# A selective scan's units doubled to half an image: in place in SBUF, its running product in four PSUM banks, the products for y gathered once a step

## The chip, the cores and the metric

The kernel runs on one NeuronCore of a Trainium2 chip. A core has a matrix engine (PE, with its weight loads shown as PEld), a vector engine (DVE), a scalar engine (ACT), a general engine (POOL) and SP, which here only issues DMA transfers. Each engine works through its own instructions in order and waits at semaphores for the others. SBUF holds the working tiles, PSUM (eight banks of 2 KB for each partition) takes what PE writes. The metric is the device time of one execution in microseconds, the median over runs. The kernel before takes 4079.44 us (three runs, 4076.0 to 4084.84).

## The reference

The input is x of shape 32 x 96 x 56 x 56, float32. Layer 0 is a ConvNeXt block (7x7 depthwise convolution, normalisation, MLP, residual). Layer 1 is a selective scan; it is the part that the change touches:

```python
x = conv_general_dilated(x, conv_w, ..., feature_group_count=C) + conv_b   # 5x5 depthwise
xs = silu(x).reshape(B, C, L)                     # L = 56*56 = 3136 tokens an image
x_dbl = einsum('kd,bdl->bkl', x_proj_w, xs)
dts, Bs, Cs = x_dbl[:, :R], x_dbl[:, R:R+N], x_dbl[:, R+N:]       # R = 6, N = 4
delta = softplus(einsum('dr,brl->bdl', dt_w, dts) + dt_b[None, :, None])
log_dA = maximum(delta[:, :, None, :] * A[None, :, :, None], LOG_EPS)      # A = -exp(A_logs)
P = exp(cumsum(log_dA, axis=-1))
dB_u = delta[:, :, None, :] * Bs[:, None, :, :] * xs[:, :, None, :]
hs = P * cumsum(dB_u / maximum(P, EPS), axis=-1)
y = einsum('bdnl,bnl->bdl', hs, Cs) + xs * Ds[None, :, None]
```

All 96 channels times 4 states are scanned along the 3136 tokens of each of 32 images.

## The kernel before

The kernel has four parts, one after the other: the first convolution, the MLP, the second convolution, and the scan, each with its own pools of tiles. The second convolution leaves silu's result in DRAM as `conv2_d`, laid out channel, image row, then all images' columns. The scan reads it from there.

In the scan, a **step** `k` is a chunk of tokens of one image and a **unit** `i` is a third of a step: 32 channels times 4 states fill the 128 partitions, so a step has NG = 3 units. A chunk is CH = 784 tokens, a quarter of an image, and NI = 4 images go side by side: steps 0 to 3 are the first quarters of images 0 to 3, steps 4 to 7 their second quarters. That makes 128 steps and 384 units. A group of NI steps shares one load of xs.

What is done for a step and its units, by function:

- `load` (L477, SP): xs for the next group, 96 partitions; each piece in DRAM is one image row of NI images, 4 x 56 floats, 896 bytes.
- `delta_in` (L495, PE) and `delta` (L506, ACT): the product of xs with a 96 x 96 matrix into PSUM, then softplus into the first half of tile `du`. Softplus needs another table in ACT than the exponential.
- `delta_x` (L523, POOL; L524, SP): delta times xs into the second half of `du`, and `du` stored to DRAM (`du_d`).
- `rows_bc` (L513, PE; L518, ACT), `spread_bc_in` (L532, PE), `spread_bc` (L542 and L543, ACT): the rows of B and C, and then B and C spread over all partitions as tiles `bt` and `ct`.
- `spread_du` (L552, SP): a unit's delta and delta*x are read back from `du_d`, each channel's row onto four partitions, as tile `rep` (two halves, four buffers).
- `decay` and `clamp` (L559, L565, L566, ACT): exp(delta*A) and two instructions that keep it above 1e-9, from `rep` into tile `da`.
- `drive` (L570, POOL): delta*x*B from `rep` into tile `u`.
- `scan` (L578, L582, L583, L587, DVE): the running product of `da` (a scan over the tokens) into PSUM tile `pv`, its last column kept in `carry_p` for the image's next chunk, the smaller of it and 1 times `u`, and the second scan into tile `hs`.
- `weigh` (L597, L599, POOL): `hs` times C into tile `hc`, and the last column of `hs` kept in `carry_h`.
- `gather` (L495 and L609, PE): D*x and the sums over the states, two matrix products a unit, into PSUM tile `py`; `store` (L618, ACT; L619, SP): `py` copied to SBUF and stored as y.

PSUM is divided into two banks for `pv`, two pairs of banks that `pz`, `pn` and `pk` take in turn (tag `bc`), and one pair for `py`.

The order on every engine is written out by hand: the loop at L631 to L667 records all instructions, and `pin` keeps them in that order on their engine. In the pass for unit `i`, `rep` is asked for unit `i + 6`, the decay and drive are done for unit `i + 3`, the scan for `i`, weigh and gather for `i - 1`. `load` stands at place 9 of a group's 12 passes, two groups ahead; softplus for a whole group stands at place 1, `delta_x` at places 1 to 4.

Of the kernel before, what the change touches and what calls it, by code (L numbers as in the profile page):

```python
# [21 lines left out]
N, R = 4, 6  # L22
# [5 lines left out]
CH = 784  # L28
NI = 4
NCH = L // CH  # L30
BK = CH // 2
# [9 lines left out]
def convnext_then_scan_kernel(  # L41
# [31 lines left out]
    du_d = dram.tile([B * NCH, C, 2 * CH], F32, name="du_d")  # L73
# [367 lines left out]
    with tc.tile_pool(name="sc", bufs=2) as pool, tc.tile_pool(  # L441
        name="sc_k", bufs=1, space=PSUM
    ) as ps_k, tc.tile_pool(name="sc_ps", bufs=2, space=PSUM) as ps_bc, tc.tile_pool(
        name="sc_y", bufs=1, space=PSUM
    ) as ps_y:
        pin = tc.keep_in_program_order

        pv = ps_k.tile([128, 1024], F32, name="pv")
        nc.vector.memset(pv, 0.0)
        zero = pv[:, 1023:1024].to_broadcast([128, CH])  # L450
# [9 lines left out]
        ready: dict = {}  # L460
        done: dict = {}
        pys: dict = {}
        pzs: dict = {}
        pks: dict = {}
        carry_p = pool.tile([128, NI * NG], F32, name="carry_p", bufs=1)
        carry_h = pool.tile([128, NI * NG], F32, name="carry_h", bufs=1)

# [4 lines left out]

        def load(p):
            b, q = place(p * NI)
            hq = H // NCH
            xt = pool.tile([C, hq, NI * W], F32, name=f"xs_{p}", tag="xs", bufs=3)
            pin(nc.sync.dma_start(  # L477
                xt,
                conv2_d[:, q * hq : (q + 1) * hq, b * W : (b + NI) * W],
            ))  # L480
            xts[p] = xt

        def tokens(k, s):

            p, i = divmod(k, NI)
            hh = H // NCH // 2
            rows = slice(s * hh, (s + 1) * hh) if s is not None else slice(None)
            return xts[p][:, rows, i * W : (i + 1) * W]
# [4 lines left out]
        def product(ps, wt, k, start=True, stop=True):  # L493
            for s in range(2):
                pin(nc.tensor.matmul(  # L495
                    half(ps, s), lhsT=wt, rhs=tokens(k, s), start=start, stop=stop
                ))

        def delta_in(k):
            pzs[k] = ps_bc.tile([128, 2, 512], F32, name=f"pz_{k}", tag="bc")  # L500
            product(pzs[k][:C], wd_t, k)

        def delta(k):
            du = pool.tile([C, 2, CH], F32, name=f"du_{k}", tag="du", bufs=5)
            o, z = two(du[:, 0, :]), pzs.pop(k)[:C, :, :BK]
            pin(nc.scalar.activation(o, z, AF.Softplus, bias=dtb_t, scale=1.0))  # L506
            dus[k] = du

        def rows_bc(k):

            pn = ps_bc.tile([128, 2, 512], F32, name=f"pn_{k}", tag="bc")
            for i in range(4):
                pin(nc.tensor.matmul(  # L513
                    half(pn[32 * i : 32 * i + 32], 0), lhsT=bcw_t, rhs=tokens(k, i % 2),
                    start=True, stop=True, tile_position=(0, 32 * i),
                ))
            bn = pool.tile([128, BK], F32, name=f"bn_{k}", tag="bn", bufs=5)
            pin(nc.scalar.copy(bn, pn[:, 0, :BK]))  # L518
            bns[k] = bn

        def delta_x(k):
            d, u = (dus[k][:, i, :].rearrange("p (h w) -> p h w", w=W) for i in range(2))
            pin(nc.gpsimd.tensor_mul(u, d, tokens(k, None)))  # L523
            pin(nc.sync.dma_start(du_d[k], dus.pop(k).rearrange("p i t -> p (i t)")))  # L524

        def spread_bc_in(k):

            bn = bns.pop(k)
            pk = [ps_bc.tile([128, 2, 512], F32, name=f"pk_{k}_{i}", tag="bc") for i in range(2)]
            for i in range(4):  # L530
                rows = slice(32 * i, 32 * i + 2 * N)
                pin(nc.tensor.matmul(  # L532
                    pk[i // 2][:, i % 2, :BK], lhsT=pick_t[rows], rhs=bn[rows],
                    start=True, stop=True, tile_position=(32 * i, 0),
                ))
            pks[k] = pk

        def spread_bc(k):
            pk = pks.pop(k)
            bt = pool.tile([128, CH], F32, name=f"bt_{k}", tag="bt", bufs=2)  # L540
            ct = pool.tile([128, CH], F32, name=f"ct_{k}", tag="ct", bufs=3)
            pin(nc.scalar.copy(two(bt), pk[0][:, :, :BK]))  # L542
            pin(nc.scalar.copy(two(ct), pk[1][:, :, :BK]))  # L543
            bts[k], cts[k] = bt, ct

        def spread_du(i):
# [3 lines left out]
            du = du_d[k, g * DG : (g + 1) * DG, :]  # L550
            src = bass.AP(du.tensor, du.offset, [du.ap[0], [0, N], *du.ap[1:]])
# [3 lines left out]
        def decay(i):  # L555

            da = pool.tile([128, CH], F32, name=f"da_{i}", tag="da", bufs=5)
            g = i % NG
            pin(nc.scalar.activation(da, reps[i][:, 0, :], AF.Exp, scale=a_t[:, g : g + 1]))  # L559
            ready[i] = da  # L560

        def clamp(i):

            da = ready[i]
            pin(nc.scalar.activation(da, da, AF.Relu, bias=lift_t[:, 0:1], scale=1.0))  # L565
            pin(nc.scalar.activation(da, da, AF.Identity, bias=lift_t[:, 1:2], scale=1.0))  # L566

        def drive(i):
            ut = pool.tile([128, CH], F32, name=f"u_{i}", tag="u", bufs=5)
            pin(nc.gpsimd.tensor_mul(ut, reps.pop(i)[:, 1, :], bts[i // NG]))  # L570
            ready[i] = ready[i], ut

        def scan(i):
            k, g = divmod(i, NG)
            (b, q), col = place(k), k % NI * NG + g
            da, ut = ready.pop(i)
# [9 lines left out]
            ht = pool.tile([128, CH], F32, name=f"hs_{i}", tag="hs", bufs=3)  # L586
# [3 lines left out]
            done[i] = ht  # L590

        def weigh(i):
            k, g = divmod(i, NG)
            q, col = place(k)[1], k % NI * NG + g
            hc = pool.tile([128, CH], F32, name=f"hc_{i}", tag="hc", bufs=3)
            ht = done.pop(i)
            pin(nc.gpsimd.tensor_mul(hc, ht, cts[k]))  # L597
            if q < NCH - 1:
                pin(nc.gpsimd.tensor_copy(carry_h[:, col : col + 1], ht[:, CH - 1 : CH]))  # L599
            done[i] = hc  # L600

        def gather(i):
            k, g = divmod(i, NG)
            if g == 0:
                pys[k] = ps_y.tile([C, 2, 512], F32, name=f"py_{k}", tag="py")
                product(pys[k], dsm_t, k, stop=False)
            hc = done.pop(i)
            for s in range(2):
                pin(nc.tensor.matmul(  # L609
                    pys[k][g * DG : (g + 1) * DG, s, :BK], lhsT=sel_t,  # L610
                    rhs=hc[:, s * BK : (s + 1) * BK], start=False, stop=True,
                    tile_position=(0, g * DG),
                ))

        def store(k):
            b, q = place(k)
            yt = pool.tile([C, CH], F32, name=f"y_{k}", tag="y")
            pin(nc.scalar.copy(two(yt), pys.pop(k)[:, :, :BK]))  # L618
            pin(nc.sync.dma_start(out[b, :, q * CH : (q + 1) * CH], yt))  # L619

        def at_step(i, fn):
            if i % NG == 0 and 0 <= i // NG < steps:
                fn(i // NG)
# [7 lines left out]
        for i in range(-10, units + 3):  # L631

            p, at = divmod(i + 10, PER)
            first = p * NI
            if at == 9 and p + 2 < PC:
                load(p + 2)
            at_unit(i + 6, spread_du)
            if i >= 2:
# [73 lines left out]
```

## Time and profile before

| | us |
|---|---|
| median of three runs | 4079.44 (4076.0 to 4084.84) |
| the profiled execution's own time | 4078.9 |
| its span, first to last instruction | 4077.1 |
| first xs load of the scan / first scan on DVE / end of the last scan | 2069.4 / 2099.3 / 4065.4 |
| DVE, POOL, ACT, PE busy between 2600 and 3000 us | 372, 343, 324, 301 of 400 |

In the page's second part the span is cut into 40 equal slices, each digit the busy share in tenths; the scan is the last 20. PEclk is the clock that PE was granted, in tenths of full speed. A group's line gives the source line, the engine, the operation, what it writes and reads with shapes, how often, then busy microseconds in all and the mean in nanoseconds of one, then the idle time of the engine just before them and what ended most of it. A table by stretches gives the busy time of PE, PEld, DVE, ACT and POOL in each stretch (number of instructions in brackets), then the granted clock from 0 to 1, the DMA engines' mean share and their rate in GB/s. A matrix product in float32 shows as two matmul instructions.

### The profile page before, as it was taken

What the parts mean: (1) busy time and instruction counts of PE and PEld (TensorE: products, weight loads), DVE (VectorE), ACT (ScalarE), POOL (GpSimd) and SP (SyncE); (2) the same over time, 40 slices, a digit from 0 to 9 for tenths busy, and PEclk for the clock granted to TensorE, in tenths of its full rate; (3) what the DMA queues carried; (4) which work ended last, traced back from release to release, by engine and by line L of the source; (5) the groups of instructions that cost most, each with busy time, mean ns of one, the idle gap of its engine ahead of it and who ended that gap; (6) DMA issues with size and microseconds to landing.
All of it is one profiled execution on the core that took longest, in us unless ns stands there. A gap on an engine that the chain in (4) does not pass through costs nothing. (4 is left out here: it accounts for less than half of the span.)

```text
span 4077.1 us, 45318 instructions
## 1 busy us (share of the span) xinstructions
PE 3340.8 (82%) x15370; PEld 1487.1 (36%) x15370; DVE 2415.9 (59%) x2181; ACT 2417.0 (59%) x2773; POOL 1965.1 (48%) x1661
## 2 busy tenths in 40 slices
PE   7999994988989888999967777777777777777775
PEld 5777771333333333666632222222222222222221
DVE  5666652222222211000039999999999999999998
ACT  3555542333333332444468877877878788787885
POOL 2333320000000000111148888888888888888886
PEclk9999996999999999999978787777778877777877
DMA  5555543444444443777777777777777777777763
GB/s 153 168 167 166 166 141 106 139 133 127 138 134 137 133 136 96 205 222 222 222 234 238 241 239 230 241 234 234 238 234 234 237 238 234 238 234 235 238 218 126
DMA packets 290731, 785.88 MB, mean 193 GB/s; under 512 B 54084, under 2 KB 161924, under 8 KB 290500
## 3 DMA queue, kind: packets, MB, share of 16 engines
q1 hardware_dynamic: 247684, 667.21, 53.4%
q0 software_dynamic: 42816, 115.77, 9.0%
q8 instruction: 122, 2.00, 0.2%
q14 instruction: 109, 0.89, 0.1%
HBM read 550.06 MB, written 232.64 MB: 192 GB/s over the span
## 5 line engine op out<-in xcount | busy, mean ns | idle before, releaser
L609 PE MATMUL py<-hc,sel_t 128*32 128x392 f32 x1536 | 736.2, 626 | 333.2 <-POOL hc L597 333.2
L597 POOL TENSOR_TENSOR hc<-hs,ct 128x784 f32<-128x784 f32 x384 | 721.6, 1879 | 294.9 <-DVE hs L587 290.7
L570 POOL TENSOR_TENSOR u<-rep,bt 128x784 f32<-128x784 f32 x384 | 716.5, 1866 | 11.2 <-DMA rep<-du_d 11.1
L356 ACT ACTIVATE g<-ph,b1p_t 128x896 f32<-128x896 f32 x336 | 320.4, 1004 | 632.9 <-PE ph L346 632.9
L269 PE MATMUL ps<-xq,wt 120*112 120x448 f32 x1536 | 581.2, 539 | 13.3 <-POOL xq L264 13.3
L578 DVE TENSOR_TENSOR_SCAN pv<-da,carry_p,pv 128x784 f32<-128x784 f32 x288 | 534.1, 1854 | 30.9 <-DVE hs L587 0.9
L587 DVE TENSOR_TENSOR_SCAN hs<-da,carry_h,pv 128x784 f32<-128x784 f32 x288 | 531.8, 1846 | 31.1 <-DVE pv L583 1.4
L365 PE MATMUL po<-g,w_t 128*32 128x448 f32 x4032 | 454.1, 588 | 98.9 <-DVE o L377 98.9
L386 POOL DMA_DIRECT2D block_d<-o x84 | 57.7, 689 | 952.5 <-DVE o L377 949.0
L269 PEld LDWEIGHTS ps<-xq,wt 120*112 120x112 f32 x1536 | 429.4, 280 | 164.7 <-POOL xq L264 13.5
L609 PEld LDWEIGHTS py<-hc,sel_t 128*32 128x32 f32 x1536 | 165.3, 129 | 862.3 <-POOL hc L597 490.8
L346 PE MATMUL ph<-h,w1r_t 32*128 32x448 f32 x4032 | 434.2, 558 | 45.0 <-DVE h L328 43.7
L416 PE MATMUL ps<-xp,wt 120*128 120x432 f32 (+1 forms) x1152 | 425.2, 533 | 18.2 <-DMA xp<-block_d 18.2
L583 DVE SCALAR_TENSOR_TENSOR pv<-pv,u 128x784 f32<-128x784 f32 x384 | 377.4, 983 | 41.5 <-DVE carry_p L582 0.9
L566 ACT ACTIVATE da<-da,lift_t 128x784 f32<-128x784 f32 x384 | 364.3, 949 | 12.9
L565 ACT ACTIVATE da<-da,lift_t 128x784 f32<-128x784 f32 x384 | 364.0, 948 | 11.8
L559 ACT ACTIVATE da<-rep,a_t 128x784 f32<-128x784 f32 x384 | 363.9, 948 | 4.9 <-DMA rep<-du_d 4.5
L328 DVE TENSOR_TENSOR h<-h,r 128x896 f32<-128x896 f32 x84 | 91.7, 1092 | 441.0 <-DMA h<-conv_d 423.2
L495 PE MATMUL py<-xs,dsm_t 96*96 96x392 f32 x512 | 311.2, 752 | 45.2 <-ACT y L618 44.9
L416 PEld LDWEIGHTS ps<-xp,wt 120*128 120x128 f32 x1152 | 289.7, 252 | 153.8 <-issue 21.8
L428 ACT ACTIVATE st<-ps,c2b_t 56x896 f32<-56x896 f32 x192 | 204.5, 1065 | 214.7 <-issue 210.3
L377 DVE SCALAR_TENSOR_TENSOR o<-po,b2r_t,x 128x448 f32<-128x448 f32 x168 | 112.3, 680 | 355.8 <-PE po L365 339.1
(84 smaller groups left out, 3318.0 us busy)
## 6 DMA issues: line engine op xcount, KB each, us to landing
rep<-du_d SPq DMA_DIRECT2D x384, 784.0 KB
du_d<-du SPq DMA_DIRECT2D x128, 588.0 KB
xt<-in_x_dram SPq DMA_DIRECT2D x192, 196.0 KB
h<-conv_d SPq DMA_DIRECT2D x84, 448.0 KB
x<-in_x_dram SPq DMA_DIRECT2D x336, 112.0 KB
block_d<-o POOLq DMA_DIRECT2D x84, 448.0 KB, 11.7
xp<-block_d SPq DMA_DIRECT2D x192, 196.0 KB
conv_d<-st POOLq DMA_DIRECT2D x96, 392.0 KB, 4.5
```

The lines of the kernel that those rows point to most:

```text
L269: nc.tensor.matmul(ps[:, j, :PQ].rearrange("p (i r) -> p i r", i=BI), lhsT=wv[:KR, t], rhs=xq[:KR, j, :, t : t + W2], start=(t == 0), stop ...
L346: pin(nc.tensor.matmul(phs[i // 2][:, i % 2, :HALF], lhsT=w1r_t[rows, d, f * 128 : (f + 1) * 128], rhs=hts[n, d][rows, s * HALF : (s + 1) ...
L365: pin(nc.tensor.matmul(po[CB * i : CB * i + CB, :HALF], lhsT=w2_t[:, f, CB * d : CB * d + CB], rhs=gts[n, s, f, i // 2][:, i % 2], start=( ...
L416: nc.tensor.matmul(ps[:, j, :PQ].rearrange("p (i r) -> p i r", i=BI)[:, :, lo:hi], lhsT=wv[:KR, t], rhs=xt[:KR, j].rearrange("p (i r) -> p ...
L565: pin(nc.scalar.activation(da, da, AF.Relu, bias=lift_t[:, 0:1], scale=1.0))
L566: pin(nc.scalar.activation(da, da, AF.Identity, bias=lift_t[:, 1:2], scale=1.0))
L570: pin(nc.gpsimd.tensor_mul(ut, reps.pop(i)[:, 1, :], bts[i // NG]))
L578: pin(nc.vector.tensor_tensor_scan(run, da, zero, carry_p[:, col : col + 1] if q else 1.0 / EPS, ALU.mult, ALU.add))
L583: pin(nc.vector.scalar_tensor_tensor(run, in0=run, scalar=1.0, in1=ut, op0=ALU.min, op1=ALU.mult))
L587: pin(nc.vector.tensor_tensor_scan(ht, da, run, carry_h[:, col : col + 1] if q else 0.0, ALU.mult, ALU.add))
L597: pin(nc.gpsimd.tensor_mul(hc, ht, cts[k]))
L609: pin(nc.tensor.matmul(pys[k][g * DG : (g + 1) * DG, s, :BK], lhsT=sel_t, rhs=hc[:, s * BK : (s + 1) * BK], start=False, stop=True, tile_p ...
```

## The change

CH becomes 1568 tokens (half an image) and NI becomes 2. So there are 64 steps and 192 units, groups of two steps and six units, and 32 groups as before.

- The running product `pv` takes four PSUM banks. The other four are two pairs that `pz`, `pn`, `pk` and now also `py` take in turn (`bank_pair`).
- The decay's three instructions write over `rep`'s first half, the drive over its second, weigh over `hs`; tiles `da`, `u` and `hc` go. `hs` has five buffers. `rep` keeps four.
- PE's and ACT's work on a step is split into halves of 784 tokens (HT) for softplus, `delta_x`, the spreads and y. `du` is stored in halves; `du_d` holds delta and delta*x of a step each in one row.
- `gather` no longer runs per unit. When a step's three units are done it makes, for each half, D*x and the six sums of the three units, whose outputs lie in different groups of columns, and stores y.
- The loop's distances change: `rep` is asked for unit `i + 3`, decay for `i + 2`, drive for `i + 1`; `load` is one group ahead at place 3 of 6; all four softplus stand at place 0, `delta_x` at places 0 to 3. Within a pass ACT's order is decay, spreads, rows, softplus, y; POOL's is weigh, drive, `delta_x`.
- A row of xs in DRAM is now 2 x 56 floats, 448 bytes.

```diff
-CH = 784
-NI = 4
+CH = 1568
+NI = 2
...
-        pv = ps_k.tile([128, 1024], F32, name="pv")
+        pv = ps_k.tile([128, 2048], F32, name="pv")
...
+        def bank_pair(name):
+            return psum.tile([128, 2, 512], F32, name=name, tag="bc")
...
+        def delta_x(k, h):
+            du = dus.pop((k, h))
+            d, u = (du[:, i, :].rearrange("p (h w) -> p h w", w=W) for i in range(2))
+            pin(nc.gpsimd.tensor_mul(u, d, tokens(k, h, 2)))
+            pin(nc.sync.dma_start(du_d[k][:, :, h * HT : (h + 1) * HT], du))
...
         def decay(i):
-            da = pool.tile([128, CH], F32, name=f"da_{i}", tag="da", bufs=5)
-            g = i % NG
-            pin(nc.scalar.activation(da, reps[i][:, 0, :], AF.Exp, scale=a_t[:, g : g + 1]))
-            ready[i] = da
+            g, da = i % NG, reps[i][:, 0, :]
+            pin(nc.scalar.activation(da, da, AF.Exp, scale=a_t[:, g : g + 1]))
...
         def drive(i):
-            ut = pool.tile([128, CH], F32, name=f"u_{i}", tag="u", bufs=5)
-            pin(nc.gpsimd.tensor_mul(ut, reps.pop(i)[:, 1, :], bts[i // NG]))
-            ready[i] = ready[i], ut
+            ut = reps[i][:, 1, :]
+            pin(nc.gpsimd.tensor_mul(ut, ut, bts[i // NG]))
...
-            ht = pool.tile([128, CH], F32, name=f"hs_{i}", tag="hs", bufs=3)
+            ht = pool.tile([128, CH], F32, name=f"hs_{i}", tag="hs", bufs=5)
...
+        def gather(k, h):
+            py = bank_pair(f"py_{k}_{h}")
+            for s in range(2):
+                pin(nc.tensor.matmul(
+                    half(py[:C], s), lhsT=dsm_t, rhs=tokens(k, 2 * h + s, 4),
+                    start=True, stop=False,
+                ))
+            for s in range(2):
+                cols = slice((2 * h + s) * BK, (2 * h + s + 1) * BK)
+                for g in range(NG):
+                    pin(nc.tensor.matmul(
+                        py[g * DG : (g + 1) * DG, s, :BK], lhsT=sel_t,
+                        rhs=hss[k * NG + g][:, cols], start=False, stop=True,
+                        tile_position=(0, g * DG),
+                    ))
...
+            pin(nc.scalar.copy(two(yt), py[:C, :, :BK]))
+            pin(nc.sync.dma_start(out[b, :, q * CH + h * HT : q * CH + (h + 1) * HT], yt))
...
+        for i in range(-12, units + 2):
+            p, at = divmod(i + 8, PER)
+            g = i % NG
+            if at == 3 and p + 1 < PC:
+                load(p + 1)
+            at_unit(i + 3, spread_du)
+            at_unit(i - 1, weigh)
+            at_unit(i + 2, decay)
+            at_unit(i + 1, drive)
+            if g == 1 and 0 <= (i + 2) // NG < steps:
+                for h in range(2):
+                    spread((i + 2) // NG, 0, h)
+            if g == 2 and 0 <= (i + 1) // NG < steps:
+                for h in range(2):
+                    spread((i + 1) // NG, 1, h)
+            if g == 2 and 0 <= (i + 4) // NG < steps:
+                rows_bc((i + 4) // NG)
+            if 0 <= p < PC and at == 0:
+                for j, h in halves:
+                    delta_in(p * NI + j, h)
+                    delta(p * NI + j, h)
+            if 0 <= p < PC and at < 4:
+                j, h = halves[at]
+                delta_x(p * NI + j, h)
+            at_unit(i, scan)
+            if g == 0 and 0 <= i // NG - 1 < steps:
+                for h in range(2):
+                    gather(i // NG - 1, h)
```

Lines of the changed kernel that the prediction speaks of: L476 loads xs, L501 is softplus, L507 delta*x, L521 the copy of the rows, L545 the read of `rep`, L551 the exponential, L564, L569 and L573 the scan's long instructions, L605 the store of y.

## The prediction

> **What bounds the kernel now.** I read the page first (busy tenths by slice), then a table by stretches of the scan stage, then the groups of instructions, then the timeline of one stretch, and last a few short stretches for the DMA rate and the clock. The change touches only the scan stage, which begins at 2069.4 us with the first load of xs and lasts to the end.
>
> ```profile
> DVE  5666652222222211000039999999999999999998
> ACT  3555542333333332444468877877878788787885
> POOL 2333320000000000111148888888888888888886
> PEclk9999996999999999999978787777778877777877
> ...
> 2600.00:3000.00 400.00, 301.20 (x962) 93.90 (x961) 372.31 (x301) 324.19 (x382) 343.30 (x250) 0.78 0.75 235
> ```
>
> From slice 21 on DVE is at 9 in every full slice. The table row (busy of PE, PEld, DVE, ACT, POOL, then granted clock, DMA share, GB/s) says 93% DVE, 86% POOL, 81% ACT, 75% PE at a clock of 0.78. The groups tell what the other 7% of DVE are:
>
> ```profile
> L578 DVE TENSOR_TENSOR_SCAN pv<-da,carry_p,pv 128x784 f32<-128x784 f32 x288 | 534.1, 1854 | 30.9 <-DVE hs L587 0.9
> L587 DVE TENSOR_TENSOR_SCAN hs<-da,carry_h,pv 128x784 f32<-128x784 f32 x288 | 531.8, 1846 | 31.1 <-DVE pv L583 1.4
> L583 DVE SCALAR_TENSOR_TENSOR pv<-pv,u 128x784 f32<-128x784 f32 x384 | 377.4, 983 | 41.5 <-DVE carry_p L582 0.9
> L566 ACT ACTIVATE da<-da,lift_t 128x784 f32<-128x784 f32 x384 | 364.3, 949 | 12.9
> L518 ACT COPY bn<-pn 128x392 f32<-128x392 f32 x128 | 58.5, 482 | 61.8 <-PE pn L513 61.8
> L542 ACT COPY bt<-pk 128x784 f32<-128x784 f32 x128 | 102.1, 797 | 44.1 <-PE pk L532 44.1
> ```
>
> DVE's idle time is 0.1 us between its own instructions; apart from one first wait of 33 us on ACT, no other engine holds it. First scan at 2099.30, last scan ends at 4065.45: 1966 us for 384 units, 5.12 each, 61.4 for twelve (four images' chunks before, a "round" of six units after). So POOL, ACT and PE may be late by some microseconds and it costs nothing. The question is whether that stays so.
>
> **The change, part by part.** A round after the change is six units: two images, half an image each; there are 32.
>
> *DVE.* A unit has the same four instructions over twice the tokens. If the 157 ns of the 128x1 carry copy (L582) are the fixed part, 784 more tokens cost 1.66 us in a scan and 0.83 in L583: 3.48 + 1.81 + 3.48 + 0.08 (half the units copy a carry) = 8.85, with 0.32 of gaps 9.17. Bounds: all fixed cost kept, 10.24; both fixed parts fully saved as taken. Six make 55.0, so DVE alone would gain 6.4 a round, 206 us.
>
> *POOL.* By its 194 ns copy as the fixed part a product over 1568 tokens costs 3.54 (bound: 3.73). Twelve, four products for u of 1.86, three carries: 50.5 a round, under 55.0.
>
> *ACT.* Copies from PSUM grow from 482 ns at 392 tokens to 797 at 784, so 784 tokens more cost about 0.65. The three decay instructions take 2.82 from start to start now, so 4.78 then (bound, doubled: 5.64). Per round: six decays 28.7, eight bt/ct copies at 0.70 5.6, two bn 1.4, four y 2.8, four softplus 3.3, two table loads at 1.30 2.6: 44.4. By sums DVE stays the bound. But ACT's order is pinned, and each of its waits below is longer than in the kernel before, since what it waits for now stands in a closed circle.
>
> *Wait 1, xs.* After SP has stored y of both halves (L605), it issues xs (L476) and only then the next rep (L545), and the queue works in order. ACT comes to that rep after one decay and two bt copies, 6.2 us after the y copy that released SP. SP's side: 2.3 of latency (the stage's first xs load took 8.04 in the chain of waits, 5.7 of it moving), 0.9 for the store of y in front, then xs, then rep. The rates, from stretches with one kind of transfer each (xs alone, then rep alone):
>
> ```profile
> 2072.00:2077.00 5.00, 0.00 (x0) 0.00 (x0) 0.00 (x0) 0.00 (x0) 0.00 (x0) 0.50 1.13 214
> 2095.00:2101.00 6.00, 0.00 (x0) 0.00 (x0) 1.70 (x1) 4.15 (x5) 3.13 (x2) 0.50 1.02 421
> ```
>
> xs now has rows of 896 bytes and moves at 214 GB/s; rep, rows of 6272, at 421. On 16 engines that is 67 ns and 238 ns a packet, a line of 39 ns + 0.032 ns per byte. xs rows shrink to 448 bytes (NI goes from 4 to 2), 168 per engine: 53 ns each, 8.9 us a load. Bounds: 5.7 if only the bytes count, 11.3 if only the packets count; I take the line, which uses both rows. rep is 1.6 MB, 3.8. Sum 2.3 + 0.9 + 8.9 + 3.8 = 15.9; ACT waits 9.7 (6.5 to 12.1). In the kernel before, rep is asked for six units ahead and ACT's wait on it is 4.9 us in all. Now the rep tile holds da and u in place, is free only after the last scan, and is asked for three units ahead; that lead of 27 us covers a plain rep (6.1) but is of no use while SP stands at the store of y.
>
> [...]
>
> *Wait 2, PE.* All products share two bank pairs, so PE may begin pn only after a ct copy, pz only after a bt copy, and ACT needs the result a copy or a table load later. Their price hangs on the clock:
>
> ```profile
> 3008.40:3017.88 9.48, 9.48 (x20) 2.55 (x20) 8.82 (x8) 6.52 (x8) 6.71 (x6) 0.50 0.49 157
> 3017.88:3024.71 6.83, 2.60 (x8) 0.67 (x8) 6.38 (x6) 3.92 (x5) 5.45 (x6) 1.00 1.10 283
> 3024.71:3031.54 6.83, 6.83 (x17) 1.89 (x16) 6.06 (x5) 5.35 (x7) 4.83 (x3) 0.50 0.79 266
> 3031.54:3045.20 13.66, 10.82 (x43) 3.93 (x41) 12.83 (x9) 13.29 (x15) 11.51 (x7) 1.00 0.57 170
> 3045.20:3052.00 6.80, 5.11 (x13) 2.03 (x14) 6.38 (x5) 5.29 (x8) 6.80 (x5) 0.50 0.95 336
> ```
>
> The clock is 0.50 or 1.00. It rises after a stretch in which PE was busy throughout, here after 9.5 and 6.8 us, and falls after one with 38% or with idle at its end. Matmul instructions follow each other at 0.33 us at full clock (four take 1.5) and 0.65 at half (2.8); with several column groups beside each other 24 took 2.34. After the change a round has some 24.6 us of PE work at full clock (four pz at 1.31, two pn at 1.55, eight pk at 0.68, four of D's products at 1.31, four times six y sums at 1.4, three columns beside each other), 49 at half, in three bursts, each begun after idle time. So I count bursts at 0.50 for their first 8.5 us:
> - bn: pn takes 3.1 + 0.3, ACT arrives after 0.7: 2.7, twice (full clock 1.0).
> - y: from pn's end D's products and the sums twice, 5.4 for the first half at 0.50, 2.7 for the second: 8.3 with 0.2 to the end, ACT there after bn, a decay and y, 6.2: 2.1, twice (0 to 4.9).
> - softplus: four pz of 2.62 behind the bt copy against 0.81 each: 0.9 + 3 x 1.8 = 6.3 (full clock 1.2).
>
> [...] The rows here show 9.5 and 6.8 us of unbroken work before the rise, so I keep the sum at 8.5.
>
> *What is queued behind.* POOL's product for u (L507) stands behind softplus, which stands behind a decay and two bt copies of the same step on ACT; POOL's next weigh, drive and so L569 on DVE stand behind it. With ACT late DVE pays at L569 and at L564.
>
> *Hidden.* SP issues 480 transfers for 672. du is stored as two rows of 3136 bytes, four units ahead. hs has five buffers and comes free with the y products, well before L573 needs it.
>
> *Start and end.* xs of the second round is now issued ahead of the first rep: 3.3 for the slower first load and about 9 for the second, so ACT's first decay moves from 2096 to 2108. The end after the last y copy stays: 4069.8 to 4077.1, 7.3.
>
> *Sum*, along ACT from its first decay: work 32 x 44.4 = 1421; xs 30 x 9.7 = 291 (two loads lie ahead of the steady rounds); bn 64 x 2.7 = 173; y 64 x 2.1 = 134; softplus 31 x 6.3 = 195: 2214. 2108 + 2214 + 7 = 4329, with the 1.8 between span and time (4077.1, 4078.9) 4331. The profiled execution is 0.5 below the median, 4079.44.
>
> **Rivals.**
> - *DVE stays the bound* (faster). It ties with today when ACT's waits are 16.4 a round (61.4, less 18 us of start and end over 32 rounds, less 44.4); I count 25.6. PE at full clock gives 9.7 + 2.0 + 1.2 = 12.9, 1421 + 291 + 64 + 37 = 1813 and so 3930; with xs at 5.7 us DVE's 55.0 decides: 4079 - 206 + 18 = 3891. For it: sums of all engines are below 55. Against: PE's work per round falls to 40% at full clock, and stretches of 38% end at 0.50.
> - *ACT bound, but cheap rows or a mixed clock*: xs at 5.7 takes 96 off, 4235; a clock that is up half the time takes off half of what full clock would (401), 4130.
> - *Half clock throughout and 11.3 a load*: y waits 4.9 (+179), xs +72: 4582. Decays at their bound would add 165 to any of these (5.2 a round).
> - *No change*: only by a balance of these.
>
> **How the numbers follow.** Forecast 4331, chance 0.55 for 4255 to 4430; half clock 0.17; cheap rows or mixed clock 0.18; DVE bound 0.08; within 0.2% (about what a measurement tells from no change, 8 us) 0.02. Slower: 0.55 + 0.17 + 0.18 = 0.90, faster 0.08. The range leaves out the DVE case and the upper half of the half-clock one: 4130 to 4490.
>
> **What would show it.** DVE busy falls to about 80% in the stage, with waits at L569 on POOL and L564 on ACT; POOL waits at L507 for softplus by some 10 us a round; ACT waits at L551 for rep some 9 us a round, at L501 for pz 6, at L521 for pn 3 twice. Granted clock in the stage below 0.78. Wrong would make it: a clock near 1.0, a rep that lands before ACT asks, or decay instructions far from 1.6 us.

## The result, and the profile after

| | before | after |
|---|---|---|
| median | 4082.14 us (4 runs) | 4185.49 us (4184.54 to 4191.64, 4 runs) |
| ratio | | 1.0258, 95% interval 1.0240 to 1.0275 |
| the profiled execution's own time, span | 4078.9, 4077.1 | 4191.64, 4189.8 |
| a round (six of the new units, twelve of the old) | 61.4 us | (4175.1 - 2117.3)/32 = 64.3 us |

The forecast, 4331, had the right sign and the right engine, but its size was wrong: 252 us more than before, where 103 were measured. The measured time lies in the stated range of 4130 to 4490, but below the 4255 to 4430 that stood for the forecast's own sum.

The busy tenths of the 40 slices, of the changed kernel:

```profile
DVE  5666651222222221000068778787787887877878
ACT  3555542333333333444466676766767667667675
POOL 2333320000000000111167878778777787787877
PEclk9999997999999998999966666666666666666666
```

Where DVE stood at 9 throughout, it is now at 7 or 8. The table by stretches, same columns as in the prediction (PE, PEld, DVE, ACT, POOL, clock, DMA share, GB/s):

```profile
2600.00:3000.00 400.00, 237.99 (x870) 77.54 (x866) 326.43 (x131) 275.93 (x232) 306.50 (x118) 0.65 0.69 228
```

No engine is over 82%: this is a kernel that waits. The groups of instructions over the whole kernel, with what ended the idle time before each, say who waits for what:

```profile
L551 ACT ACTIVATE rep<-rep,a_t 128x1568 f32<-128x1568 f32 x192 | 307.7, 1603 | 218.3 <-DMA rep<-du_d 215.5 <-DVE hs L573 2.4
L604 ACT COPY y<-py 96x784 f32<-96x784 f32 x128 | 103.2, 806 | 179.5 <-PE py L597 177.7
L521 ACT COPY bn<-pn 128x784 f32<-128x784 f32 x64 | 52.0, 812 | 142.2 <-PE pn L515 142.2
L501 ACT ACTIVATE du<-pz,dtb_t 96x784 f32<-96x784 f32 x128 | 116.3, 909 | 98.7 <-PE pz L493 97.8 <-issue 0.9
```

ACT pays 215.5 us for `rep`, 177.7 for y's sums, 142.2 for `bn` and 97.8 for Softplus. It is busy 1111 of the 1600 us between 2200 and 3800, 44.7 a round, 1430 in 32. Work and waits (`rep` without the 13.6 ahead of the first decay) make 2049 of the 2074 us from the first decay (2112.4) to the end of the last y copy (4186.4); the rest, 25 us, is what is left between its 1209 instructions, 21 ns for each. So the chain that I had summed is the one that sets the end. DVE's idle time is passed on to it: 293 us at L569 behind POOL, 65 at L564 behind ACT.

One round in the timeline (start, duration, engine, line; in brackets the idle time and what ended it), first the Softplus burst, then the queue of SP around xs:

```profile
3018.40 7.71 PE L493 MATMUL pz<-xs,wd_t 96*96 96x392 f32 x16 [4.54 <-ACT bt L537]
3021.36 0.91 ACT L501 ACTIVATE du<-pz,dtb_t 96x784 f32<-96x784 f32 x1 [1.01 <-PE pz L493]
3022.35 1.84 POOL L507 TENSOR_TENSOR du<-du,xs 96x784 f32<-96x784 f32 x1 [14.30 <-ACT du L501]
...
3031.13 1.80 DVE L569 SCALAR_TENSOR_TENSOR pv<-pv,rep 128x1568 f32<-128x1568 f32 x1 [9.59 <-POOL rep L557]
...
3043.39 3.75 SPq L605 DMA_DIRECT2D out_dram<-y  x2
3045.99 0.81 ACT L604 COPY y<-py 96x784 f32<-96x784 f32 x1 [2.62 <-PE py L597]
...
3047.24 0.38 SPq L476 DMA_DIRECT2D xs<-conv_d  x1
3047.71 3.47 SPq L545 DMA_DIRECT2D rep<-du_d  x1
...
3059.49 1.60 ACT L551 ACTIVATE rep<-rep,a_t 128x1568 f32<-128x1568 f32 x1 [6.52 <-DMA rep<-du_d]
```

The reader is to see two chains. ACT's first Softplus is late, POOL has stood 14.30 us at the product that needs it, and DVE stands 9.59 us for POOL. And SP sends the y store, xs and `rep` in that order: from the end of the y copy (3046.80) to the decay that needs `rep` it takes 12.69 us, 6.52 of them idle on ACT.

### The profile page after: what moved, and what is told of

Same layout as the page of the kernel before. It is cut to its first block, busy times and chain, and to the rows that moved or that the text cites. A ratio compares the mean times of both kernels' runs of the same rounds, so it can differ in the third digit from the quotient of the medians.

```text
span 4189.8 us, 41783 instructions
## 1 busy us (share of the span) xinstructions
PE 3145.8 (75%) x15370; PEld 1451.1 (35%) x15370; DVE 2272.1 (54%) x1413; ACT 2278.5 (54%) x2133; POOL 1867.9 (45%) x1085
## 4 chain that ended last, share of the span: by engine, by line
POOL 18%; issue 17%; DVE 8%; DMA 5%; ACT 2%; PE 1%; POOLq 0%; DVEq 0%; SPq 0%; ACTq 0%
POOL rep L557 9%; POOL hs L584 6%; DMA rep<-du_d 4%; DVE hs L573 3%; POOL du L507 3%; DVE pv L564 3%; DVE pv L569 2%; ACT rep L551 1%; ACT rep L552 1%; ACT ct L537 1%; DMA xs<-conv_d 0%; PE pz L493 0%; PE py L597 0%; PE py L590 0%; POOL carry_h L583 0%
## 5 line engine op out<-in xcount | busy, mean ns | idle before, releaser
L584 POOL TENSOR_TENSOR hs<-hs,ct 128x1568 f32<-128x1568 f32 x192 | 672.7, 3504 | 50.9 <-ACT ct L537 32.6
L557 POOL TENSOR_TENSOR rep<-rep,bt 128x1568 f32<-128x1568 f32 x192 | 672.7, 3504 | 6.8 <-ACT bt L537 6.8
L270 PE MATMUL ps<-xq,wt 120*112 120x448 f32 x1536 | 582.1, 540 | 13.2 <-POOL xq L265 13.2
L569 DVE SCALAR_TENSOR_TENSOR pv<-pv,rep 128x1568 f32<-128x1568 f32 x192 | 345.5, 1800 | 311.0 <-POOL rep L557 293.2
L507 POOL TENSOR_TENSOR du<-du,xs 96x784 f32<-96x784 f32 x128 | 236.3, 1846 | 464.9 <-ACT du L501 464.9
L551 ACT ACTIVATE rep<-rep,a_t 128x1568 f32<-128x1568 f32 x192 | 307.7, 1603 | 218.3 <-DMA rep<-du_d 215.5
L533 PE MATMUL pk<-bn,pick_t 8*128 8x392 f32 x1024 | 275.5, 634 | 167.6 <-ACT bt L537 152.6
L493 PE MATMUL pz<-xs,wd_t 96*96 96x392 f32 x512 | 249.7, 658 | 169.5 <-ACT bt L537 155.1
L564 DVE TENSOR_TENSOR_SCAN pv<-rep,pv 128x1568 f32<-128x1568 f32 x96 | 329.1, 3428 | 62.1 <-ACT rep L553 55.7
L564 DVE TENSOR_TENSOR_SCAN pv<-rep,carry_p,pv 128x1568 f32<-128x1568 f32 x96 | 334.9, 3488 | 16.4 <-ACT rep L553 9.8
L573 DVE TENSOR_TENSOR_SCAN hs<-rep,carry_h,pv 128x1568 f32<-128x1568 f32 x96 | 334.0, 3480 | 10.0
L573 DVE TENSOR_TENSOR_SCAN hs<-rep,pv 128x1568 f32<-128x1568 f32 x96 | 328.4, 3421 | 9.6
```

The costliest lines, as they stand in the source:

```text
L270: nc.tensor.matmul(ps[:, j, :PQ].rearrange("p (i r) -> p i r", i=BI), lhsT=wv[:KR, t], rhs=xq[:KR, j, :, t : t + W2], start=(t == 0), stop ...
L507: pin(nc.gpsimd.tensor_mul(u, d, tokens(k, h, 2)))
L551: pin(nc.scalar.activation(da, da, AF.Exp, scale=a_t[:, g : g + 1]))
L557: pin(nc.gpsimd.tensor_mul(ut, ut, bts[i // NG]))
L564: pin(nc.vector.tensor_tensor_scan(run, da, zero, carry_p[:, col : col + 1] if q else 1.0 / EPS, ALU.mult, ALU.add))
L569: pin(nc.vector.scalar_tensor_tensor(run, in0=run, scalar=1.0, in1=ut, op0=ALU.min, op1=ALU.mult))
```

## The experiments

Ratios are to runs of the kernel before on the same chip. The last two columns are from the stretch 2200 to 3800 us: ACT's wait for `rep`, and how long DVE was busy of 1600.

| kernel | us | ratio, 95% interval | rep wait | DVE |
|---|---|---|---|---|
| after, for comparison | 4185.49 | 1.0258, 1.0240 to 1.0275 | 165.7 | 1307 |
| 1 `du` products a pass later | 4184.97 | 1.0243, 1.0223 to 1.0262 | 164.1 | 1304 |
| 2 xs behind rep | 4085.85 | 1.0002, 0.9993 to 1.0012 | 84.8 | 1376 |
| 3 copies behind the next decay | 4070.82 | 0.9967, 0.9955 to 0.9979 | 166.5 | 1390 |
| 4 edits 2 and 3, Softplus earlier | 4059.26 | 0.9943, 0.9920 to 0.9966 | 224.3 | 1391 |
| 5 rep first in SP's queue | 3981.01 | 0.9753, 0.9721 to 0.9785 | 0.0 | 1455 |
| 6 edits 1, 3 and 5, Softplus earlier | 3901.13 | 0.9557, 0.9529 to 0.9584 | 16.2 | 1530 |
| 7 xs in one row a channel | 4144.82 | 1.0155, 1.0127 to 1.0184 | 113.6 | 1331 |
| 8 PE kept busy, 24 products | 4251.34 | 1.0407, 1.0370 to 1.0443 | 43.0 | 1246 |
| 9 edits 5 and 1 | 3983.44 | 0.9763, 0.9745 to 0.9781 | 0.0 | 1455 |
| 10 edits 5 and 3 | 3912.85 | 0.9588, 0.9567 to 0.9609 | 27.8 | 1525 |
| 11 PE kept busy, 8 products | 4162.76 | 1.0205, 1.0178 to 1.0233 | 160.5 | 1319 |

The column for `rep` has the idle time that the profile puts down to the DMA. In kernels 3, 4, 7 and 11 another 12, 9, 33 and 13 us ahead of the same decay are put down to DVE or POOL; in 7 they stand at the same place of the round and are as long (5.43 and 5.45 beside 5.34 and 5.49), so its wait is rather 146.8.

**1. Is POOL behind Softplus the bound?** My theory says ACT is; the rival reads the 14.3 us at L507 as the cause.

```diff
-            if 0 <= p < PC and at < 4:
-                j, h = halves[at]
-                delta_x(p * NI + j, h)
+            p1, at1 = divmod(i + 7, PER)
+            if 0 <= p1 < PC and at1 < 4:
+                j, h = halves[at1]
+                delta_x(p1 * NI + j, h)
```

> The four products for u (L507) stand one pass later in POOL's order, so POOL does its weigh and drive before it waits for softplus. Nothing on ACT, PE or SP's loads moves. Theory ACT (ACT's own order is the closed circle: y copy, SP, xs, rep, decay, with PE's answers inside it; POOL and DVE only follow): the round stays at 64.3 us, the time within 0.5% of the changed kernel's 4185, and DVE's 280 us of waiting at L569 for POOL moves to the first scan, waiting for ACT. Rival POOL (the 14 us that POOL stands at L507 for softplus each round are what sets the pace): 8 to 9 us a round go, 32 rounds, 3900 to 3930, where DVE's 55 decide.

4184.97: no change from 4185.49. DVE's groups between 2200 and 3800 us (in the changed kernel the first of them waits 232.2 for POOL, the other two 8.2 and 11.4 for ACT):

```profile
L569 DVE SCALAR_TENSOR_TENSOR pv<-pv,rep 128x1568 f32<-128x1568 f32 x148 | 266.3, 1800 | 71.8 <-POOL rep L557 60.8 <-POOL hs L584 0.5 <-DVE pv L564 0.5
L564 DVE TENSOR_TENSOR_SCAN pv<-rep,carry_p,pv 128x1568 f32<-128x1568 f32 x76 | 265.1, 3488 | 102.7 <-ACT rep L553 100.2
L564 DVE TENSOR_TENSOR_SCAN pv<-rep,pv 128x1568 f32<-128x1568 f32 x73 | 250.3, 3429 | 103.3 <-ACT rep L553 100.7 <-DVE hs L573 0.4
```

DVE's wait was only renamed, from POOL to ACT. POOL was the messenger.

**2. What does xs ahead of rep cost?**

```diff
-            if at == 3 and p + 1 < PC:
+            if at == 3 and p + 1 < PC and i < 0:
                 load(p + 1)
             at_unit(i + 3, spread_du)
+            if at == 4 and p + 1 < PC and i >= 0:
+                load(p + 1)
```

> The load of xs moves one pass back and behind that pass's rep in SP's order, so that no rep which ACT soon needs stands behind it in the queue. Theory ACT with the xs term: ACT's 6.7 us a round of waiting for rep fall to about 1, the round goes to 58 to 61.5 us (the PE waits may grow where the clock is low), 3985 to 4095. Rival POOL: no change, 4185. Rival that rep is late because DVE frees its tile late, with xs by chance in front: the wait falls by 2 us at most, 4120 or more.

4085.85, 99.6 us less than the changed kernel, and ACT's wait for `rep` is halved (165.7 to 84.8). I had expected about 1 us a round to be left; 3.3 are (84.8 in 26 rounds). So xs ahead of `rep` accounts for half of the wait. The other half is there without it.

**3. What do ACT's waits for PE cost?** The copy of `bn` and the copy of y's second half move behind ACT's next decay, which runs while PE works (`rows_out` and `store` hold the copies that `rows_bc` and `gather` ended with; `store` sends y as well).

```diff
+            if g == 0 and 0 <= (i + 3) // NG < steps:
+                rows_out((i + 3) // NG)
+            if g == 1 and 0 <= (i - 1) // NG - 1 < steps:
+                store((i - 1) // NG - 1, 1)
...
-                for h in range(2):
-                    gather(i // NG - 1, h)
+                gather(i // NG - 1, 0)
+                store(i // NG - 1, 0)
+                gather(i // NG - 1, 1)
```

> ACT's copy of the rows (bn) and of y's second half move behind the next unit's decay, so PE has 4.8 us longer for each; xs stays where it is. Theory ACT with PE waits: 4.5 us a round at bn and 5.0 at y, some of it comes back at y's first half, where PE is still at half clock: the round falls by 2 to 5 us, 4030 to 4120, and ACT's wait for rep stays at about 6. Rival POOL or rival xs alone: no change, 4185.

4070.82, 114.7 less than the changed kernel and slightly below the kernel before. `bn` no longer waits; 3.6 us a round are gained, less than its 4.4, since a wait of 1.4 a round for `bt` is new.

**4. Do the gains add up?** Edits 2 and 3 together, and Softplus ahead of the `bt` copies in its pass.

```diff
+            if 0 <= p < PC and at == 0:
+                for j, h in halves:
+                    delta_in(p * NI + j, h)
+                    delta(p * NI + j, h)
             if g == 1 and 0 <= (i + 2) // NG < steps:
                 for h in range(2):
                     spread((i + 2) // NG, 0, h)
...
-            if 0 <= p < PC and at == 0:
-                for j, h in halves:
-                    delta_in(p * NI + j, h)
-                    delta(p * NI + j, h)
```

> e2 and e3 together, and softplus ahead of the bt copies on ACT. Theory ACT: its work of 45 us and what is left of the waits (8 to 10) come under DVE's 55 us a round, so DVE is the bound again with gaps of 0.1 us: a round of 54.5 to 55.5, 3870 to 3910, 5% below the kernel before. Rival POOL: POOL still stands at L507, 64 a round, 4185.

They don't: 4059.26 (runs from 4038 to 4076), far from the 3870 to 3910 that I expected. ACT's wait for `rep` grew to 224.3. The timeline of this kernel, SP's queue beside ACT's decays:

```profile
3000.30 0.56 SPq L550 DMA_DIRECT2D rep<-du_d  x1
3000.95 1.77 SPq L478 DMA_DIRECT2D xs<-conv_d  x1
...
3003.70 8.97 SPq L550 DMA_DIRECT2D rep<-du_d  x1
...
3012.02 1.60 ACT L556 ACTIVATE rep<-rep,a_t 128x1568 f32<-128x1568 f32 x1 [4.76 <-DMA rep<-du_d]
...
3018.32 0.32 SPq L614 DMA_DIRECT2D out_dram<-y  x1
3018.75 0.51 SPq L550 DMA_DIRECT2D rep<-du_d  x1
3021.53 1.60 ACT L556 ACTIVATE rep<-rep,a_t 128x1568 f32<-128x1568 f32 x1 [3.24 <-DMA rep<-du_d]
```

DVE frees a `rep` buffer at 3012.8, but SP asks for its next content at 3018.75, since the store of y that stands ahead waits for ACT's copy (3017.49). And the issue behind xs is held for 8.97 us. So either the queue's order or the transfer rate is at fault. The next edit separates them.

**5. The order of the queue.** In each pass `rep` goes first; the stores of `du` and y that a pass has made are sent behind the next pass's `rep`, and xs behind these (`late` is the list that the stores are put on).

```diff
+        def send():
+            while late:
+                pin(nc.sync.dma_start(*late.pop(0)))
...
-            if at == 3 and p + 1 < PC:
-                load(p + 1)
             at_unit(i + 3, spread_du)
+            send()
+            if at == 4 and p + 1 < PC and i >= 0:
+                load(p + 1)
```

> The changed kernel with one edit in the order of SP's queue: each pass's `rep` load is issued first, and the stores of `du` and of `y` that stood ahead of the next pass's load, and the `xs` load, go behind it. Theory (order of the queue): a `rep` load's buffer is free long before SP issues it, because a store of `y` that waits for ACT's copy or a store of `du` that waits for POOL's product stands ahead. Between 2200 and 4000 us ACT waited 186.6 us for `rep`; moving `xs` alone behind took that to 97.6 and 100 us off the time. With the stores behind as well it should fall under 50 and the time to 4030-4060 us. Rival (bandwidth): the loads are short of transfer rate, not of an early issue; then the wait stays near the 98 of the `xs` edit and the time near its 4086. Rival (cover): `du` now reaches memory a pass later, and the first `rep` of a unit waits for it: 4086 or more.

3981.01: 204.5 us less than the changed kernel and 2.5% faster than the kernel before, beyond what either theory gave it. The groups between 2200 and 3800 us:

```profile
L570 DVE SCALAR_TENSOR_TENSOR pv<-pv,rep 128x1568 f32<-128x1568 f32 x166 | 298.8, 1800 | 108.5 <-POOL rep L558 93.0 <-DVE carry_p L569 0.9 <-DVE pv L565 0.5
L552 ACT ACTIVATE rep<-rep,a_t 128x1568 f32<-128x1568 f32 x166 | 266.3, 1604 | 0.3
```

ACT's wait for `rep` is gone, though the same bytes move, and at a higher DMA share (0.78 of the stretch against 0.68). The gain is the size of the whole wait of the steady rounds (215.5 less the first 13.6, 202). It was order, not rate. Which of the stores counted was not tried apart: in the changed kernel, between 2200 and 3800 us, SP stood 641 us at the stores of y, for ACT, and 614 at those of `du`, for POOL.

**6. All of it.** Edit 5 with edits 1 and 3 and the earlier Softplus.

> The edit of the queue's order together with the copies of `bn` and of `y`'s second half behind the next unit's decay, Softplus ahead of the `bt` copies, and POOL's `du` products one pass later, so that POOL no longer waits for Softplus. Theory: with ACT's rep waits (6.7 a round), its waits for `bn` and `y` (2 x 2.2 and 2 x 2.5) and POOL's wait for Softplus gone, a round is DVE's own 55.0 to 57 us against 64.3; 32 rounds give back 235-300 us: 3890-3950 us. Rival (transfers): the four edits without the queue's order and without the later products gave 4059, because `rep` loads came late through back-pressure beside `xs`; if that is bandwidth and not order, this stays at 4030-4070 with ACT still waiting some 200 us for `rep` in the 1800 us between 2200 and 4000.

3901.13, ratio 0.9557: the fastest kernel of the study. The table by stretches:

```profile
2200.00:3800.00 1600.00, 1171.13 (x4178) 378.87 (x4176) 1530.43 (x611) 1301.24 (x1102) 1432.45 (x549) 0.66 0.80 263
```

DVE is busy 96% of the stage at a clock as low as in the changed kernel (0.66), and a round is (3886.4 - 2112.6)/32 = 55.4 against the 55.0 that were forecast for DVE alone with its gaps; its instructions are 53.0 of it. So half an image per unit does save DVE's time, as its sums say; the change lost it in ACT's and SP's order.

**9 and 10. Which of these edits paid, once `rep` is first?** ACT's round in kernel 5 is 45 of work and waits of 4.9 for y, 4.5 for `bn`, 3.0 for Softplus, near its 58.1.

> The kernel with `rep` first in SP's queue (3981.0 us), and POOL's `du` products one pass later; the copies stay where the change put them. In the `rep`-first kernel ACT no longer waits for `rep`, and its round is its own work of some 45.1 us, 2 x 2.9 of waits for the sums of `y`, 2 x 2.2 for `bn` and 2.9 for Softplus: 58.2, the round's length (32 rounds from 2117 to 3974 us are 58.0 each). Theory (ACT is the bound there): POOL's wait for Softplus (243.6 us between 2200 and 4000) is cover, and taking it away gives nothing: 3970-3990. Rival (POOL behind Softplus is the bound, since DVE waits 99.6 us for POOL's `drive` in that stretch): 32 rounds by some 2.5 us, 3895-3920.

> The kernel with `rep` first in SP's queue (3981.0 us), and the copies of `bn` and of `y`'s second half behind the next unit's decay; Softplus and POOL's products stay where the change put them. Theory (ACT is the bound there): ACT's waits for `bn` (2 x 2.2 a round) and for one of the two `y` halves (some 2.9, twice a round) go, its round falls from 58.2 under DVE's own 55.0, and the time is 3900-3930, near the 3901 of all edits together. Rival (POOL behind Softplus): the time stays above 3950, and only all edits together reach 3901.

The later `du` products gave nothing again (3983.44): DVE's wait for POOL at L570 fell from 93.0 to 36.7 us, and 61 us of waiting for ACT at L565 came in its place. The later copies gave 68 us (3912.85), near the 3901 of all edits; the intervals of the two ratios, 0.9567 to 0.9609 and 0.9529 to 0.9584, overlap. Kernel 10, between 2200 and 3800 us:

```profile
L557 ACT ACTIVATE rep<-rep,a_t 128x1568 f32<-128x1568 f32 x173 | 277.8, 1606 | 28.1 <-DMA rep<-du_d 27.8
L510 POOL TENSOR_TENSOR du<-du,xs 96x784 f32<-96x784 f32 x116 | 213.9, 1844 | 165.2 <-ACT du L504 165.2
```

POOL still stands 165 us behind Softplus there, with DVE at 95%: that idle time cost nothing there. Both theories' numbers came in as ACT-bound says.

**7. Does the row length set the price of xs?** The prediction's line says that 448-byte rows cost 8.9 us a load. This kernel loads as many bytes to the same tile, but tokens from other places of the images; its y is not the reference's, and only its time is of use.

```diff
-                xt, conv2_d[:, q * HQ : (q + 1) * HQ, b * W : (b + NI) * W]
+                xt.rearrange("c h w -> c (h w)"),
+                conv2_d.rearrange("c h w -> c (h w)")[
+                    :, p * HQ * NI * W : (p + 1) * HQ * NI * W
+                ],
```

> The changed kernel, with each `xs` load reading one contiguous stretch of 12,544 bytes a channel instead of 28 rows of 448 bytes; as many bytes to the same tile at the same place in the queue, but the tokens are taken from other places of the images, so the output is not the reference's. Theory (rows): the load's time hangs on its row length. Alone it took some 6.0 us with 448-byte rows; at the 421 GB/s of the 6272-byte rows before the first unit it would take 2.9, so ACT's wait for the `rep` load behind it (6.7 us a round) falls by up to 3.1 and the time by 60-95 us: 4090-4125. Rival (bytes alone): row length is without effect, and the time stays at 4185 within 6.

4144.82, 40.7 less: between the two theories. The first load of the stage has the chip to itself. The changed kernel, issue and the first product that needs it:

```profile
2077.50 0.31 SPq L476 DMA_DIRECT2D xs<-conv_d  x1
2084.97 5.51 PE L493 MATMUL pz<-xs,wd_t 96*96 96x392 f32 x8 [13.84 <-DMA xs<-conv_d]
```

and the kernel with one row of 12,544 bytes a channel:

```profile
2063.68 0.32 SPq L476 DMA_DIRECT2D xs<-conv_d  x1
2071.05 10.33 PE L496 MATMUL pz<-xs,wd_t 96*96 96x392 f32 x16 [13.74 <-DMA xs<-conv_d]
```

7.47 us against 7.37: alone, the row length is worth 0.1 us. In the rounds, with `rep` right behind it, the median from the issue of xs to the decay that waited for that `rep` is 12.2 with short rows and 11.3 with long ones; about 1 us a round, 30 of the 41. (Short rows keep the DMA engines busy 0.97 of the time for 188 GB/s, 2079 to 2085 us; the long row 0.66 for 171, 2065 to 2071. That the transfer which shares these engines pays for this would fit the 1 us, but was not tried apart.)

**8 and 11. Is it the clock?** In the changed kernel the bursts begin at half clock: between 2200 and 3800 us all 49 that begin with `pn` and all 25 that begin with `pz` (the last one's rise lies past 3800) found it at 0.50. 24 products of no use (KB), or 8, are put between those for `bt` and those for `pz`, where PE is idle.

```diff
+            if (kind, h) == (0, 1):
+                for s in range(KB):
+                    pin(nc.tensor.matmul(
+                        pk[:, s % 2, BK:], lhsT=w1_t[:, :128], rhs=w1_t[:, : 512 - BK],
+                        start=True, stop=True,
+                    ))
```

> The changed kernel with 24 more products of 128 columns by 120 on PE, right behind those of `bt`'s second half, into columns that nobody reads, in the stretch where PE otherwise waits for ACT's copies just ahead of the burst for `pz`. Theory (clock): the Softplus waits (3.15 us a round after the first) are long because the burst begins at a granted clock near 0.5-0.6; if PE is kept busy ahead of it the burst starts at 1.0, the wait falls to some 1.5 and the time by 30-60 us: 4125-4155. Rival (order): the waits are PE's order behind ACT's copies and not its clock; the time stays at 4185, or rises by what the added products delay (24 of 0.1-0.25 us in every second pass that they run past the copy, to 4230).

> The changed kernel with 8 instead of 24 of the added products, which end before ACT's copy comes (16 instructions of 0.2-0.37 us in a gap of some 4.5 us), so that they delay nothing. With 24 the granted clock stood at 1.0 for 6.85 us at a time and then at 0.50 for some 13 us, while PE was busy without a gap, so business of PE does not raise it. Theory (the clock does not follow PE's business): Softplus waits stay near 3 us a round and the time at 4185 within 10. Rival (business ahead of a burst raises the clock): 4125-4155.

With 24 it took 4251: they run 9 us, longer than I had counted, and hold the `bt` copy back by 4.6 us twice a round, so that the time is above both theories' numbers. But they show something of the clock. Two stretches that follow each other in that kernel:

```profile
3027.10:3033.90 6.80, 6.69 (x44) 3.17 (x39) 6.71 (x2) 4.70 (x5) 2.75 (x1) 1.00 0.41 122
3034.00:3047.20 13.20, 13.20 (x46) 9.87 (x45) 8.88 (x5) 6.38 (x7) 2.18 (x2) 0.50 0.26 104
```

PE is busy without a gap for 13.2 us, after 6.7 of 6.8 us at full clock, and is granted 0.50 the whole time. So in this stretch being busy was not enough.

It mattered which products ran. In the traces' records of the clock, any two changes in this stage are a whole multiple of 3.413 us apart (between 2200 and 3800 us 148 changes in the changed kernel and 202 in the kernel before; in steps of 3.4133 us none is off by more than 0.005). Cut into windows by this grid, the 13.2 us are two windows of the added products alone, one of added products and `pz`, and one of `pz` alone; the clock is 1.00 right behind the last. In the changed kernel, between 2200 and 3800 us, the windows at 0.50 that were followed by 1.00 are these (full means that PE was busy for at least 99.5% of the window; the added products of kernel 8 write to `pk`):

| windows at 0.50 | changed kernel | kernel 8 | kernel before |
|---|---|---|---|
| full, products for `pz` and y alone | 74 of 74 | 66 of 68 | 59 of 60 |
| full, products for `pn` or `pk` among them | 0 of 49 | 0 of 156 | 16 of 66 |
| not full | 0 of 198 | 0 of 93 | 26 of 78 |

So in this stretch of the changed kernel the clock rose behind a full window of `pz` or y products, 74 times, and behind none of the 247 others; in the kernel before this is less strict (42 of 144 others). Why some products count and others don't was not tried.

With 8 products, which delay nothing, the Softplus wait is 76.6 us between 2200 and 3800 (75.5 without), and the time 4162.76, 23 us less. The time lies between the two theories' numbers: the Softplus wait speaks for the first; what fell is the wait for y (124.9 to 100.0), and why is open.

## Why the prediction was right or wrong

- *DVE's sums* were right: 3.43 to 3.49, 1.80 and 3.42 to 3.48 us for the three long instructions (3.48, 1.81, 3.48 forecast), a decay instruction 1.60, a POOL product 3.50 (3.54). Kernel 6 runs at 55.4 a round; 55.0 was forecast for DVE alone.
- *The bound moves to ACT*: right; kernels 1, 5, 9 and 10 show it. The chain Softplus, POOL, L569 was as I wrote, and kernels 1 and 9 show that it is a consequence and no cause.
- *Wait 1, the xs term*, is the first step that failed. The line through two rates made 8.9 us of a load with 448-byte rows, 2.3 + 8.9 = 11.2 with the latency; the first load of the stage took 7.47 from issue to use (kernel 7 above). With its lower bound, bytes alone at 214 GB/s, the same sum is 2.3 + 0.9 + 5.7 + 3.8 = 12.7, and the timeline has 12.69. ACT waited 202 in the steady rounds where I had 291. The fault was to put the 421 GB/s of `rep` down to its row length: a load of xs in rows of 12,544 bytes took 7.37 us against 7.47 (kernel 7). Why `rep` moves faster alone was not tried.
- *The same step's cause* was half the truth. I put the whole wait on xs. Moving xs gives 100 us back (kernel 2), moving the stores as well 204 (kernel 5). I had written that `rep`'s lead "is of no use while SP stands at the store of y", and priced only the load behind that store. The lead itself was misread: its 27 us reach to the scan, but ACT's decay comes one pass after `rep` is asked for, a sixth of the round or 10.7 us, where it came three passes after in the kernel before (3 x 5.12 = 15.4). So what holds SP in any one pass soon reaches ACT.
- *The rows themselves*: those of 448 bytes moved at 188 GB/s with the tail of the load in it, with the DMA engines busy 0.97 of the time (2079 to 2085 us), against 214 at 1.13 for 896 bytes (the prediction's row of the kernel before): for each byte the engines were about as busy in both. One row of 12,544 bytes took less of them (171 at 0.66) and landed no sooner (7.37 us against 7.47).
- *Wait 2, Softplus*, is the second: 97.8 us where I had 195. I counted all four `pz` at half clock, 2.62 each; in the round shown the burst of four takes 7.71 in all, 1.93 each, because the clock rises in its midst, at about 3022.9. The three waits behind the first are 1.24, 0.41 and 0.46 there and not 1.8. `bn` was nearly right (2.2 for 2.7), y a little low (177.7 in all for 134).
- *The clock term* behind it was 0.50 for the first 8.5 us of every burst. Between 2200 and 3800 us that was nearly right where a burst begins with `pn`: the clock rose after 9.15 us (median of 49 bursts). The Softplus burst begins with `pz`, and there it rose after 4.51 (median of 24). That the clock is up after a stretch of unbroken work was read from two rows, of 9.5 and 6.8 us. The windows under 8 show 74 rises in the changed kernel right behind one full window of 3.413 us, and 49 full windows there and 156 in kernel 8 without a rise behind them: not all unbroken work counted. The mean clock between 2600 and 3000 us came out at 0.65, as forecast below 0.78.
- *The sum*: of the 140 us between forecast and trace from first decay to last y copy (2214 and 2074), xs is 89, Softplus 97, `bn` 31; against that y 44, ACT's work 9 and the small gaps 25. Two sizes were off in the same direction. The true size lies in the rival "cheap rows or a mixed clock", 4130 to 4235, which had both causes in its name. In part that is luck: it priced them one at a time, and both together would have been 4331 - 96 - 200 = 4035. The waits for PE fell by 84 us (97 + 31 - 44), where the rival's half of full clock took off 200.

## What to carry to other kernels

When a change takes slack from a load (here `rep` is asked for one pass ahead of its decay instead of three), look first at the queue that issues it: a load whose buffer is free must not stand behind a store that waits for another engine. That one reordering turned 2.6% slower into 2.5% faster. And take waits off in the order of the chain: the same edit (POOL's products later) was worth nothing twice, because ACT was the bound both times, and an engine that idles 14 us in front of an instruction may only be handing on somebody else's delay.

## What was unexpected of the hardware

- The granted clock of PE was 1.00 for 6.83 us at a time in the changed kernel's scan (74 times between 2200 and 3800 us), from about 3009.2, 3022.9 and 3043.4 us for instance, so 13.7 and 20.5 apart, and 0.50 between. Its 148 changes in that stretch lie on a grid of 3.413 us; it rose behind all 74 windows of the grid that products for `pz` and y filled, and behind none of the 247 others at 0.50. In the same stretch its mean was 0.65 to 0.68 in the changed kernel and its variants, with PE busy from 971 to 1313 of the 1600 us, and 0.78 in the kernel before, with 1189. What makes it fall, and why it did not rise behind the 49 full windows with `pn` or `pk`, is open.
- The rounds of some of these kernels kept step with this grid. From one group's Softplus to the next, past the first rounds, it is 58.02 to 58.15 us in kernel 5 and 58.02 to 58.06 in kernel 9, 17 steps of 3.413; in the changed kernel and kernel 1 the mean is 64.86 and 64.85, 19 steps. So the 204.5 us of edit 5 are also 30 rounds of two steps (205), and a gain below a step might not show: "nothing" in kernels 1 and 9 rests on the waits, which moved from POOL to ACT, more than on the time. Whether the grid draws the rounds to itself was not tried.
- Rows of 448 bytes and rows of 12,544 bytes load the same 1.2 MB in the same time when alone (7.47 and 7.37 us from issue to first use), while they keep the DMA engines busy for 0.97 and 0.66 of the 6 us read off (2079 to 2085 and 2065 to 2071 us).
- The issue of a `rep` load that follows xs and another `rep` was held for 9 us in SP's queue (8.97 and 9.88 in kernel 4), where the other `rep` issues between 3000 and 3066 us took 0.51 to 0.56. That is time in which SP issued nothing else: behind the 8.97 that begin at 3003.70 its next issue is at 3018.32.
